# Reordering key sums, transposes and input copies, and giving GpSimd 144 of 384 columns of a product, in an attention and state-space kernel

## The chip, the cores and the metric

The kernel runs on one core of a Trainium2 chip. The metric is the device time of one execution in microseconds; the median of several executions is compared. Engine names are those of the profile: PE is TensorE (PEld its weight loads), DVE is VectorE, ACT is ScalarE, POOL is GpSimd, SP is SyncE, which here issues all DMAs.

## The reference, cut to what matters

The input is 8 samples of 512 channels by 48 x 48 = 2304 positions, all float32. Two layers follow each other, each adding to its own normalised input: a causal linear attention with 8 heads, and a chain of four selective state-space blocks ("Mamba") of 128 channels each.

```python
x = x + _L0_conv_ref(_gn(x), Wq, bq, Wkv, bkv)      # layer 0
x = x + _L1_conv_ref(_gn(x), ...)                   # layer 1
# layer 0: Q = elu(q)+1, K = elu(k)+1
den = 1.0 / (einsum('nhld,nhld->nhl', Q, cumsum(K, axis=1)) + 1e-10)
S = S + k[..., :, None] * v[..., None, :];  o = einsum('nhk,nhkv->nhv', q, S)   # per position
# layer 1, four times (channels i*128 ..), each on its own 128 channels plus the last result:
xs = silu(causal_conv4(u @ Wi_x.T) + bc);  z = u @ Wi_z.T
delta = softplus(dt @ Wdt.T + bdt);  A = -exp(A_log)
h = exp(delta * A) * h + (delta * xs) * B_t;  y_t = sum_n h * C_t               # per position, 256 x 16 states
x_m = ((y + xs * D) * silu(z)) @ Wo.T
fused = w_local * x_i + w_global * maximum(x_i, x_m)
```

Note the cumulative sum of K: the key as it comes out of its projection is summed by head over the heads' channels and over what lies before, and is multiplied with the query.

## The kernel before, in words

**Tiling.** Positions are cut into six chunks of 384 (`LC`). Layer 0 is a list of 8 x 4 x 6 = 192 calls of `chunk` (sample, group of 128 channels, chunk of positions). Layer 1 is a list of 192 jobs (class `Job`): sample, block, chunk of positions. Two streams of samples alternate, so that while one stream's job is scanned, the next one of the other is prepared.

**A job and its slots.** A job's 256 channels x 16 states are scanned in 8 slots (`SLOTS`) of 4 scans. Channels come in halves of 128: slots 0 to 3 are half 0, slots 4 to 7 half 1. A slot goes as follows. The product u = B x (delta xs) is made in two parts: `last_product` (L857) lets POOL make the last `TAIL` = 128 columns of each of the four rows (L864), `product` (L872) lets DVE make the first 256 (L875), which read delta xs from a copy in PSUM, `dxp`, that ACT makes in `inputs` (L845, L848) once per half from the loaded tile `dxr`. Then four scans on DVE (`scan`, L896) each take one decay row exp(delta A), which ACT has written to a PSUM bank (`decay`, L885). Then POOL multiplies with C (`weigh`, L908), and PE sums over states into the PSUM tile `yp` (`gather`, L924). `skip` (L850, L853) starts a half's sum: ACT writes xs x D over `yp`, which DVE must have read before (`gated`, L936, tile `yz`).

**The order is written out by hand.** `slot(k)` (L1145) issues what belongs to slot k: first the DVE product of slot k+1, then `gated` if it is due (half 1 of the job before at s = 2, half 0 at s = 6), then the background work of this half slot (`beside(2k)`), then four times: a scan, in slots 2 and 6 after the first one the `skip`, and `ahead(DEPTH)`, which issues decays until 3 are in hand. After the second scan come the copies of the last columns (`keep`, L919), one `gather`, `inputs`, `last_product` of slot k+2, and the second half's background work, `beside(2k+1)`. At s = 6 it is the `inputs(0)` of the next job, at s = 2 the `inputs(1)` of this one. At s = 7 the DVE product of the next job's slot 1 is issued here too, right after slot 7's second scan.

**Background work** is a set of generators: `chunk` for layer 0, `Job.prepare` (L688) for the next jobs, statistics, and the hand-over between blocks (`pass_on`). Each `yield` names the half slot at which the next step is due and how many PSUM banks it needs. In `chunk`, `at(j)` means j half slots after the chunk's start; in `prepare`, `first` is the half slot at which its job is first scanned. A chunk's start lies, for nearly all chunks, 3 half slots after a job's start. So a step at `at(9)` falls into the first half of slot 6, `at(10)` into its second half, and the job being prepared has `first - 21` in the second half of slot 5 (first convolution, L700), `first - 19` in the second half of slot 6 (second convolution and gate, L700 and L711) and `first - 18` at the start of slot 7 (four Silus, L736 to L741, between two loads of ACT's function tables). A softplus (L771) has two more loads.

**Banks.** Six PSUM banks (`BANKS`) are shared by the decays (3 to 5), the projections, the transposes and the convolutions. A bank is handed out in the program's order; whoever writes it next waits for who read it last.

**Queues that matter here.** Each engine runs its instructions in the order of issue. SP issues the loads of `prepare`: `steps` (dr), `scaled` (dxr), `rows` (B and C), two DMAs each, after `spread` has stored `delta` and `dx` to DRAM; `save`d stores are flushed at certain points. In a chunk, `kc` are the key sums (L381, L383), `kept` their copy for the next group (L387), `pr` the product with the query on DVE (L391), `turned` the transposed keys and values (L398), `kl` and `v` their copies to SBUF by ACT (L402, L403).

Of the kernel before, what the change touches and what calls it, by code (L numbers as in the profile page):

```python
# [19 lines left out]
LC = 384  # L20
NG = 2
SLOTS = 8
TAIL = 128
BANKS = 6
DEPTH = 3
LEAD = 11
# [24 lines left out]
def attention_then_mamba_kernel(  # L51
# [12 lines left out]
    nc = tc.nc  # L64
# [17 lines left out]
    ident = cst[:, C_ID : C_ID + P]  # L82
# [3 lines left out]
    k_tri = cst[:, C_TRI : C_TRI + P]  # L86
# [86 lines left out]
    def save(out, in_):  # L173
        stores.append((half_no[0], out, in_))

    def flush(every=True):
        while stores and (every or stores[0][0] <= half_no[0] - 2):
            _, o, i = stores.pop(0)
            nc.sync.dma_start(out=o, in_=i)
# [103 lines left out]
    def chunk(m):  # L283


        b, o, c = parts[m]
        n = f"{b}_{o}_{c}"
        bank = Banks()
# [5 lines left out]
        def at(j, gap=1):  # L294
            return times[m] + j, gap

        def new(tag, bufs=1, shape=(P, LC)):
            return apool.tile(list(shape), F32, tag=tag, name=f"{tag}_{n}", bufs=bufs)

        def project(j):  # L300
            ps = bank()[:, 0:LC]
            for kt in range(4):
                nc.tensor.matmul(  # L303
                    ps,
                    wqs[m // NC][:, kt, j * P : (j + 1) * P],
                    xn[:, kt, :],
                    start=(kt == 0),
                    stop=(kt == 3),
                )
            return ps, bqkv_sb[:, j * 4 + o : j * 4 + o + 1]  # L310
# [42 lines left out]
        if o:  # L353
            before = new("before")
# [14 lines left out]
        k = new("k", 2)  # L369
        nc.vector.scalar_tensor_tensor(k, ex, 1.0, kp, ALU.min, ALU.add)  # L370
        bank.free()
        yield at(4, 0), 1
        vp, vb = project(2)
        yield at(6), 0
        vT = new("vT")
        nc.scalar.activation(vT, vp, AF.Identity, bias=vb)
        bank.free()

        yield at(7), 1
        kc = bank()[:, 0:LC]  # L380
        nc.tensor.matmul(kc, k_tri, k, start=True, stop=(o == 0))  # L381
        if o:
            nc.tensor.matmul(kc, ident, before, start=False, stop=True)  # L383
        yield at(8), 0
        if ksum is not None:
            kept = new("before")
            nc.scalar.copy(kept[64:128], kc[64:128])  # L387
            save(ksum[:, cols], kept[64:128])
        yield at(9), 0
        pr = new("pr")  # L390
        nc.vector.tensor_mul(pr, q, kc)  # L391
        bank.free()
        yield at(9, 0), 2
        turned = []
        for src in (k, vT):
            ps = bank()[:, 0:LC].rearrange("p (i t) -> p i t", i=NT)
            for i in range(NT):
                nc.tensor.transpose(ps[:, i, :], src[:, subs[i]], ident)  # L398
            turned.append(ps)
        yield at(10), 0  # L400
        kl, v = new("kl", 1, (P, NT, P)), new("v", 2, (P, NT, P))
        nc.scalar.copy(kl, turned[0])  # L402
        nc.scalar.copy(v, turned[1])  # L403
# [42 lines left out]
        for sc in scs:  # L446
# [4 lines left out]
                start=True,  # L451
                stop=False,
                skip_group_check=True,
            )
        for i in range(NT):
            for h, sc in zip(heads_of, scs):
# [4 lines left out]
                    start=False,  # L461
                    stop=i == NT - 1,
# [12 lines left out]
        for i in range(NT):  # L475
            old = c > 0 or i > 0
            for h, sm in zip(heads_of, sms):
                if old:
# [4 lines left out]
                        start=False,  # L483
                        stop=False,
                        skip_group_check=True,
                    )
            for h, sm in zip(heads_of, sms):
# [4 lines left out]
                    start=False,  # L492
                    stop=i == NT - 1,
# [187 lines left out]
    class Job:  # L681
# [6 lines left out]
        def prepare(self):  # L688
# [3 lines left out]
            wk, s = self.w = st.w  # L692
            self.state, self.fsum, self.fm = st.state, st.fsum, st.fm
            xi, c0 = st.xi, c * LC
            bank = Banks()
# [28 lines left out]
            first = 2 * self.start  # L724
# [64 lines left out]
            def pairs(t, rows):  # L789
                for i in range(2):  # L790
                    nc.sync.dma_start(out=t[i * 64 : i * 64 + 64], in_=rows)

            def steps(h):
                self.dr[h] = drs[h]
                pairs(self.dr[h][:, :, 1 : 1 + LC], dsrc[h])

            def scaled(h):
                self.dxr[h] = mpool.tile([P, 2, LC], F32, tag="dxr", name=f"dxr_{n}_{h}")
                pairs(self.dxr[h], xsrc[h])

            def rows(m, q):
                t = mpool.tile([P, NG, LC], F32, tag="BC"[m], name=f"{'BC'[m]}_{n}_{q}", bufs=4)
                for i in range(2):
                    nc.sync.dma_start(  # L804
                        out=t[i * 64 : i * 64 + 64].rearrange("p j l -> p (j l)"),
                        in_=src[q, m, i].partition_broadcast(64),
                    )
                (self.B, self.C)[m][q] = t
# [8 lines left out]
            yield first - 7, 0  # L817
            flush()
            steps(0)
            rows(0, 0)  # L820
            yield first - 6, 0
            scaled(0)
            yield first - 5, 0
            rows(0, 1)
            self.prepared = True
# [19 lines left out]
        def inputs(self, h):  # L845

            self.dxp = psx.tile([P, 2, LC - TAIL], F32, tag="dxp", name=f"dxp_{self.n}_{h}")
            nc.scalar.copy(self.dxp, self.dxr[h][:, :, 0 : LC - TAIL])  # L848

# [7 lines left out]
        def last_product(self, s):  # L857

            shape, cols = [P, NG, 2, TAIL], slice(LC - TAIL, LC)
            u = mpool.tile([P, NG, 2, 1 + LC], F32, tag="u", name=f"u_{self.n}_{s}", bufs=5)  # L860
            if self.c:
                h, q = s // 4, s % 4 * NG
                nc.scalar.copy(u[:, :, :, 0], self.state[:, h, q : q + NG, :])
            nc.gpsimd.tensor_tensor(  # L864
                u[:, :, :, 1 + LC - TAIL :],
                self.B[s % 4][:, :, cols].unsqueeze(2).to_broadcast(shape),
# [5 lines left out]
        def product(self, s, u):  # L872

            shape, cols = [P, NG, 2, LC - TAIL], slice(0, LC - TAIL)
            nc.vector.tensor_mul(  # L875
                u[:, :, :, 1 : 1 + LC - TAIL],
                self.B[s % 4][:, :, cols].unsqueeze(2).to_broadcast(shape),
# [104 lines left out]
    slots = SLOTS * len(jobs)  # L982
# [45 lines left out]
    def finale(job):  # L1028
        yield "0", 1
        job.project()  # L1030
        yield "1", 0
        job.maximum()
        if job.c == NC - 1:
            yield from job.stream.pass_on()
# [4 lines left out]
    for b in counted:  # L1039
        first = times[parts.index((b, 0, 0))]  # L1040
# [23 lines left out]
    def beside(half):  # L1064

        half_no[0] = half
        flush(every=False)
        begin(half // 2 + LEAD)

        for t in heads:  # L1070
            if t.need is not None and t.need[1] == 0 and t.fits() and t.due():
                t.step()
        held = False
        for t in tasks + heads:
            while t.need is not None and t.due():
                if not t.fits() or held and t.need[1]:
                    held = held or t.need[1] > len(spare)
                    break
                t.step()
        prune()  # L1080
# [19 lines left out]
    def at(k):  # L1100
        return jobs[k // SLOTS], k % SLOTS

    def apart(k):

        return k % SLOTS == 0 and k > 0 and at(k)[0].c == 0 and at(k)[0].stream is at(k - 1)[0].stream
# [5 lines left out]
    def ahead(n):  # L1111

        nonlocal todo
        while len(decays) < n and spare and todo < 4 * slots:
            k = todo // 4
            if apart(k) and k not in primed:
                break
            job, s = at(k)
            if not job.prepared or s // 4 not in job.dr:
                break  # L1120
            decays.append(job.decay(s, todo % 4))
            todo += 1
# [22 lines left out]
    def slot(k):  # L1145
        job, s = at(k)
        end = k + 1 == slots or apart(k + 1)
        if not end and k + 1 not in drawn:
            j, r = at(k + 1)
            j.product(r, us[k + 1])  # L1150
        before = jobs[k // SLOTS - 1] if k >= SLOTS else None
        if s == 2 and before is not None and not before.closed:
            before.gated(1)
            tasks.insert(0, Task(finale(before)))
        elif s == 6:
            job.gated(0)
        beside(2 * k)
        for i in range(4):
            job.scan(s, i, us[k], decays.pop(0))
            if i == 0 and s in (2, 6):  # L1160
                job.skip(s // 4)
            ahead(DEPTH)
            if i == 1:

                while kept:
                    kept.pop(0)()
                if len(waiting) > 1:
                    waiting.pop(0)()
                if s == 2:
                    job.inputs(1)  # L1170
                elif s == 6 and k + 2 < slots and not apart(k + 2):
                    j = at(k + 2)[0]
                    if not j.prepared:
                        hurry(k + 2, lambda: j.prepared)
                    j.inputs(0)
                if not end and k + 2 < slots and not apart(k + 2):
                    j, r = at(k + 2)
                    us[k + 2] = j.last_product(r)
                    if s == 7:

                        j.product(r, us[k + 2])
                        drawn.add(k + 2)
                beside(2 * k + 1)
        u = us[k]
        job.weigh(s, u)
        kept.append(lambda: at(k)[0].keep(s, u))
        waiting.append(lambda: at(k)[0].gather(s, us.pop(k)))
        if end:
            close(k)
            if k + 1 < slots:  # L1190
                prime(k + 1)
            else:
                hurry(slots, lambda: not tasks)
                flush()
# [101 lines left out]
```

## Time and profile before

| | |
|---|---|
| median of 3 runs | 8580.44 us (8571.5 to 8580.68) |
| the profiled execution | 8565.29 us, its span 8563.5 us |
| busy: PE, DVE, ACT, POOL | 7704.4, 8067.9, 6845.7, 7758.3 us |
| scans (L896), 6144 | 5457.8 us busy, 940 ns each |
| decays (L885), 6144 | 3412.3 us busy, 578 ns each |
| ACT table loads (L885, L736, L771) | 1283 ns each, 192 of L736 |
| idle of PE ahead of the convolutions (L700) | 215.6 us, of which 163.1 until ACT's copy kl |
| TensorE clock granted | 0.973 of full |

The page gives busy time by engine, then groups of equal instructions: line, engine, operation, tile written <- tiles read, size, count; after the first bar the busy time in us and the mean of one in ns; after the second the engine's idle time just before, and what ended most of it. Consecutive DVE and ACT instructions overlap by some tens of ns, so count times mean is a little over the busy time. The table of waits reads: engine, tile and line that waited, <- what ended the wait: us in total, times, longest. The timeline gives start, length, instruction, and in brackets the idle time ahead of it. The profiled execution is one execution; it was 15 us under the median.

### The profile page before, as it was taken

What the parts mean: (1) busy time and instruction counts of PE and PEld (TensorE: products, weight loads), DVE (VectorE), ACT (ScalarE), POOL (GpSimd) and SP (SyncE); (2) the same over time, 40 slices, a digit from 0 to 9 for tenths busy, and PEclk for the clock granted to TensorE, in tenths of its full rate; (3) what the DMA queues carried; (4) which work ended last, traced back from release to release, by engine and by line L of the source; (5) the groups of instructions that cost most, each with busy time, mean ns of one, the idle gap of its engine ahead of it and who ended that gap; (6) DMA issues with size and microseconds to landing.
All of it is one profiled execution on the core that took longest, in us unless ns stands there. A gap on an engine that the chain in (4) does not pass through costs nothing. (4 is left out here: it accounts for less than half of the span.)

```text
span 8563.5 us, 124248 instructions
## 1 busy us (share of the span) xinstructions
PE 7704.4 (90%) x36482; PEld 3691.2 (43%) x36482; DVE 8067.9 (94%) x11078; ACT 6845.7 (80%) x14438; POOL 7758.3 (91%) x4235
## 2 busy tenths in 40 slices
PE   8899999999999999999899999999899999999975
PEld 4444444444444444444444444444444444444422
DVE  2899999999999999999999999999999999999998
ACT  3788888878888888878888888888788888888875
POOL 1789999999999999999999999999999999999998
PEclk9999999999999999999999999999999999999977
DMA  5667777767766777777777677777777676666665
GB/s 186 172 185 191 200 203 195 201 194 203 207 192 190 198 202 204 200 192 197 200 203 196 192 190 203 202 200 194 199 202 201 192 194 190 187 191 190 180 162 148
DMA packets 974424, 1654.36 MB, mean 193 GB/s; under 512 B 119337, under 2 KB 768169, under 8 KB 973618
## 3 DMA queue, kind: packets, MB, share of 16 engines
q1 hardware_dynamic: 973746, 1646.43, 69.8%
q8 instruction: 290, 4.75, 0.2%
q14 instruction: 388, 3.18, 0.1%
HBM read 1318.28 MB, written 327.68 MB: 192 GB/s over the span
## 5 line engine op out<-in xcount | busy, mean ns | idle before, releaser
L896 DVE TENSOR_TENSOR_SCAN u<-bank,u 128x385 f32<-128x385 f32 (+1 forms) x6144 | 5457.8, 940 | 254.2 <-ACT bank L885 253.8
L908 POOL TENSOR_TENSOR u<-u,C 128x1536 f32<-128x1536 f32 x1536 | 4889.0, 3183 | 606.8 <-DVE u L896 284.9
L885 ACT ACTIVATE bank<-dr,scales 128x385 f32<-128x385 f32 (+1 forms) x6144 | 3412.3, 578 | 700.6 <-DVE u L896 598.1
L924 PE MATMUL yp<-u,cst 128*64 128x384 f32 x12288 | 2368.3, 506 | 176.5 <-POOL u L908 91.3
L864 POOL TENSOR_TENSOR u<-B,dxr 128x512 f32<-128x512 f32 x1536 | 1965.5, 1280 | 19.6 <-DMA dxr<-xscr 17.0
L875 DVE TENSOR_TENSOR u<-B,dxp 128x1024 f32<-128x1024 f32 x1536 | 1837.7, 1196 | 10.0 <-ACT dxp L848 10.0
L303 PE MATMUL bank<-xn,wq 128*128 128x384 f32 x4608 | 1721.9, 518 | 66.3 <-DVE u L896 41.3
L924 PEld LDWEIGHTS yp<-u,cst 128*64 128x64 f32 x12288 | 773.4, 138 | 1365.7 <-issue 897.5
L700 PE MATMUL bank<-xi,wk 128*128 128x384 f32 x3072 | 1123.9, 509 | 215.6 <-ACT kl L402 163.1
L303 PEld LDWEIGHTS bank<-xn,wq 128*128 128x128 f32 x4608 | 862.0, 197 | 837.9 <-DVE u L896 128.4
L700 PEld LDWEIGHTS bank<-xi,wk 128*128 128x128 f32 x3072 | 563.5, 193 | 780.5 <-ACT kl L402 274.1
L315 ACT ACTIVATE ex<-bank,bqkv_sb 128x384 f32<-128x384 f32 x384 | 221.0, 576 | 447.5 <-PE bank L303 447.5
L885 ACT ACT_TABLE_LOAD x382 | 490.1, 1283 | 6.8
L853 ACT ACTIVATE yp<-xs,scales 128x384 f32<-128x384 f32 x384 | 223.4, 582 | 316.7 <-DVE yz L936 316.7
L813 POOL TENSOR_TENSOR dx<-delta,xs 128x384 f32<-128x384 f32 x384 | 385.5, 1004 | 22.3 <-ACT delta L771 22.3
L435 PE MATMUL bank<-cst,rdb 128*128 128x128 f32 x576 | 100.7, 284 | 262.0 <-DVE u L896 260.0
L942 PE MATMUL bank<-yz,scales 128*128 128x384 f32 x768 | 303.2, 511 | 32.4 <-DVE yz L936 21.3
L760 PE MATMUL bank<-dbc,steps_w 9*128 9x384 f32 x768 | 301.2, 511 | 3.0 <-ACT dbc L752 3.0
L711 PE MATMUL bank<-xi,scales 128*128 128x384 f32 x768 | 288.6, 497 | 11.0 <-ACT xs L736 11.0
L747 PE MATMUL bank<-xs,scales 128*40 128x384 f32 x768 | 280.8, 488 | 2.7 <-ACT sm L469 2.7
L488 PE MATMUL bank<-sm,v 128*64 128x128 f32 x2304 | 256.0, 301 | 0.0
L736 ACT ACT_TABLE_LOAD x192 | 246.3, 1283 | 3.5
(117 smaller groups left out, 7866.5 us busy)
## 6 DMA issues: line engine op xcount, KB each, us to landing
B<-scr SPq DMA_DIRECT2D x1536, 192.0 KB, 4.3
C<-scr SPq DMA_DIRECT2D x1536, 192.0 KB, 4.7
xn<-xn SPq DMA_DIRECT2D x192, 768.0 KB, 7.1
dr<-dscr SPq DMA_DIRECT2D x768, 192.0 KB, 3.8
dxr<-xscr SPq DMA_DIRECT2D x768, 192.0 KB, 4.9
dscr<-delta SPq DMA_DIRECT2D x192, 384.0 KB, 6.8
xscr<-dx SPq DMA_DIRECT2D x192, 384.0 KB, 2.4
xn<-in_x SPq DMA_DIRECT2D x48, 768.0 KB, 6.4
```

The source lines that it names most:

```text
L303: nc.tensor.matmul(ps, wqs[m // NC][:, kt, j * P : (j + 1) * P], xn[:, kt, :], start=(kt == 0), stop=(kt == 3),)
L700: nc.tensor.matmul(xc, wk[:, k, h * P : (h + 1) * P], xi[:, c0 + k : c0 + k + LC], start=(k == 0), stop=(k == 3),)
L711: nc.tensor.matmul(zp, w_gate[:, s, h * P : (h + 1) * P], xi[:, c0 + 3 : c0 + 3 + LC], start=True, stop=True,)
L760: nc.tensor.matmul(vp, steps_w[32:41, s, h * P : (h + 1) * P], dbc[32:41, :], start=True, stop=True)
L813: nc.gpsimd.tensor_tensor(dx[:, h, :], delta[:, h, :], xs[:, h, :], ALU.mult)
L864: nc.gpsimd.tensor_tensor(u[:, :, :, 1 + LC - TAIL :], self.B[s % 4][:, :, cols].unsqueeze(2).to_broadcast(shape), self.dxr[s // 4][:, :, ...
L875: nc.vector.tensor_mul(u[:, :, :, 1 : 1 + LC - TAIL], self.B[s % 4][:, :, cols].unsqueeze(2).to_broadcast(shape), self.dxp.unsqueeze(1).to ...
L885: nc.scalar.activation(dA[:, cols], self.dr[h][:, g, cols], AF.Exp, scale=w_a[:, self.w[1], 2 * h + g, q + j : q + j + 1],)
L896: nc.vector.tensor_tensor_scan(u[:, j, g, cols], dA[:, cols], u[:, j, g, cols], 0.0, ALU.mult, ALU.add,)
L908: nc.gpsimd.tensor_tensor(u[:, :, :, 0:LC], u[:, :, :, 1:], self.C[s % 4].unsqueeze(2).to_broadcast([P, NG, 2, LC]), ALU.mult,)
L924: nc.tensor.matmul(self.yp[g * 64 : g * 64 + 64, 0:LC], pair_sum, u[:, j, g, 0:LC], start=False, stop=(s % 4 == 3 and j == NG - 1), skip_g ...
L942: nc.tensor.matmul(self.xm[:, 0:LC], w_out[:, self.w[1], h, :], self.yz[:, h, :], start=(h == 0), stop=(h == 1),)
```

## The change

`TAIL` goes from 128 to 144: POOL makes 144 columns of each row of the product with B, DVE 240, and `dxp` is two rows of 240.

In `chunk` the key sums move from `at(7)` to `at(5)`, ahead of vT's bias on ACT; the copy `kept` follows vT at `at(6)` (before: `at(8)`); `pr` moves from `at(9)` to `at(7)`, the transposes from `at(9, 0)` to `at(7, 0)`, and the copies `kl` and `v` from `at(10)` to `at(9)`, the first half of slot 6.

In `prepare` the load of the first `dxr` moves from `first - 6` to `first - 7`, and the first rows of B from `first - 7` to `first - 6`.

In `slot`, at s = 6, the next job's `inputs(0)` is issued after the first scan and ahead of `skip`, if that job is prepared by then; otherwise after the second scan, as before.

```diff
-TAIL = 128
+TAIL = 144
...
         yield at(4, 0), 1
         vp, vb = project(2)
+        yield at(5), 1
+        kc = bank()[:, 0:LC]
+        nc.tensor.matmul(kc, k_tri, k, start=True, stop=(o == 0))
+        if o:
+            nc.tensor.matmul(kc, ident, before, start=False, stop=True)
         yield at(6), 0
         vT = new("vT")
         nc.scalar.activation(vT, vp, AF.Identity, bias=vb)
         bank.free()
-
-        yield at(7), 1
-        kc = bank()[:, 0:LC]
-        nc.tensor.matmul(kc, k_tri, k, start=True, stop=(o == 0))
-        if o:
-            nc.tensor.matmul(kc, ident, before, start=False, stop=True)
-        yield at(8), 0
         if ksum is not None:
             kept = new("before")
             nc.scalar.copy(kept[64:128], kc[64:128])
             save(ksum[:, cols], kept[64:128])
-        yield at(9), 0
+        yield at(7), 0
         pr = new("pr")
         nc.vector.tensor_mul(pr, q, kc)
         bank.free()
-        yield at(9, 0), 2
+        yield at(7, 0), 2
         turned = []
...
-        yield at(10), 0
+        yield at(9), 0
         kl, v = new("kl", 1, (P, NT, P)), new("v", 2, (P, NT, P))
...
             yield first - 7, 0
             flush()
             steps(0)
+            scaled(0)
+            yield first - 6, 0
             rows(0, 0)
-            yield first - 6, 0
-            scaled(0)
...
             if i == 0 and s in (2, 6):
+                j = at(k + 2)[0] if s == 6 and k + 2 < slots and not apart(k + 2) else None
+                early = j is not None and j.prepared
+                if early:
+                    j.inputs(0)
                 job.skip(s // 4)
...
-                elif s == 6 and k + 2 < slots and not apart(k + 2):
+                elif s == 6 and not early and k + 2 < slots and not apart(k + 2):
```

## The prediction

> **What bounds the kernel now.** I read the page's engine line and groups first, then who waited for whom, then the timeline of one job (eight slots of four scans) engine by engine, then the busy time of whole jobs.
>
> ```profile
> PE 7704.4 (90%) x36482; PEld 3691.2 (43%) x36482; DVE 8067.9 (94%) x11078; ACT 6845.7 (80%) x14438; POOL 7758.3 (91%) x4235
> ...
> L908 POOL TENSOR_TENSOR u<-u,C 128x1536 f32<-128x1536 f32 x1536 | 4889.0, 3183 | 606.8 <-DVE u L896 284.9
> ...
> L864 POOL TENSOR_TENSOR u<-B,dxr 128x512 f32<-128x512 f32 x1536 | 1965.5, 1280 | 19.6 <-DMA dxr<-xscr 17.0
> L875 DVE TENSOR_TENSOR u<-B,dxp 128x1024 f32<-128x1024 f32 x1536 | 1837.7, 1196 | 10.0 <-ACT dxp L848 10.0
> ```
>
> DVE is the fullest engine. Its 495.6 us of idle time are the start (about 180), and this, from the table of waits:
>
> ```profile
> ACT yp L853 <- DVE yz L936: 316.7, 203, 3.5
> DVE u L896 <- ACT bank L885: 253.8, 192, 3.8
> PE bank L700 <- ACT kl L402: 163.1, 161, 1.7
> ```
>
> The scans wait for a decay 192 times, and there are 192 jobs: one stop of 1.32 us in each. The timeline shows its place; first DVE, then ACT, same job:
>
> ```profile
> 2572.19 0.55 DVE L936 TENSOR_TENSOR yz<-yp,sz 128x384 f32<-128x384 f32 x1
> 2572.66 0.54 DVE L391 TENSOR_TENSOR pr<-q,bank 128x384 f32<-128x384 f32 x1
> 2573.12 3.50 DVE L896 TENSOR_TENSOR_SCAN u<-bank,u 128x385 f32<-128x385 f32 x4
> 2576.54 1.20 DVE L875 TENSOR_TENSOR u<-B,dxp 128x1024 f32<-128x1024 f32 x1
> ...
> 2583.57 2.66 DVE L896 TENSOR_TENSOR_SCAN u<-bank,u 128x385 f32<-128x385 f32 x3 [1.68 <-ACT bank L885]
> ```
>
> ```profile
> 2572.78 0.58 ACT L853 ACTIVATE yp<-xs,scales 128x384 f32<-128x384 f32 x1 [1.47 <-DVE yz L936]
> ...
> 2575.66 0.58 ACT L848 COPY dxp<-dxr 128x512 f32<-128x512 f32 x1
> 2576.18 0.19 ACT L863 COPY u<-state 128x4 f32<-128x4 f32 x1
> 2576.39 0.48 ACT L402 COPY kl<-bank 128x384 f32<-128x384 f32 x1
> 2576.77 0.49 ACT L403 COPY v<-bank 128x384 f32<-128x384 f32 x1
> 2577.14 1.11 ACT L885 ACTIVATE bank<-dr,scales 128x385 f32<-128x385 f32 x2
> 2578.27 1.28 ACT L736 ACT_TABLE_LOAD   x1
> ```
>
> The reader is to see: ACT sits idle for 1.47 us ahead of the skip term, then does dxp, kl and v, and only then the two decays and the switch to Silu. From the load at 2578.27 to the last scan of slot 7 at 2583.57 lie 5.30 us in which ACT delivers nothing that DVE can scan with; DVE's own work ends 1.68 us short of that. So the length of a job (42.6 to 42.7 us in most) is set by a loop: DVE up to the last scan of slot 6, then ACT through the Silu stage. Two other engines stand close. Busy time of two whole jobs:
>
> ```profile
> 2552.60:2595.30 42.70, 39.20 (x192) 18.87 (x192) 40.92 (x55) 35.99 (x80) 38.94 (x21) 1.00 0.72 195
> 2120.00:2162.60 42.60, 38.83 (x193) 18.61 (x192) 41.16 (x61) 35.20 (x71) 42.40 (x27) 1.00 0.58 161
> ```
>
> Columns from the third: PE, weight load, DVE, ACT, POOL. In the usual job POOL has 3.8 us to spare (39 to 40 us busy in seven of ten jobs); in the second kind, where it also normalises chunks for a new sample, 0.2. I count 38 jobs of 41.4 us or more.
>
> **What the Trainium skill says.** (1) "GPSIMD Engine Reference", Elementwise side-by-side cycle accounting: a two-input op costs about 2.6 cycles an element at 1.2 GHz, 2.17 ns. The trace agrees: 730, 1004 and 1280 ns for 256, 384 and 512 elements (L543, L813, L864) are 2.15 ns each more; only L908 is flatter (1.86 from 512 to 1536). (2) The same page, Key points: GpSimd and VectorE contend where a DVE instruction has two SBUF inputs. Here the DVE product reads dxp from PSUM, and L864 keeps within 1251 to 1328 ns, so the trace shows little of it. (3) "ScalarE: Activation LUTs", What ACT_TABLE_LOAD costs: 1283 ns, the trace's 1283; its further drain of 1380 ns does not show, Silu starts 1.29 us after the load (2579.56).
>
> **The change, part by part.** *144 columns for GpSimd.* 64 elements leave the DVE product. From yz (384: 552 ns) to the product (1024: 1196 ns), both with a PSUM input, is 1.006 ns an element: 64.4 ns x 1536 = **98.9 us off DVE**. POOL gets 64 x 2.15 = 137 ns x 1536 = 211 us (low end 1.86 ns: 183; high end in proportion to 1280/512: 246), so 1.10 us a job (0.95 to 1.28). In the usual job this lies in the 3 to 4 us of spare; in the full ones it is on the path. The dxp copies shorten by 24 ns each (581 for 512 against 484 for 384), 9 us of ACT: counted as nothing.
>
> *Copies and inputs ahead of the skip term.* In the built order of the changed kernel, ACT does kl, v, dxp, skip, then decay, decay, state copies, decay, decay, table load, in nearly every job. kl and v (0.86 us back to back) fit the 1.47 us in which ACT stood idle. dxp must wait until the DVE product ahead of yz has read the old dxp (2572.19), so it ends some 0.1 us after yz; the skip behind it, and PE's gather behind that, are late by that much, and the next decay only has to be there for the scan 2.6 us later. If that cover is gone dxp costs 0.58. The fourth decay takes the bank of slot 6's last scan, so it starts at 2576.6 and not at 2577.7; the load follows at 2577.2, not 2578.27: **1.07 us earlier**. DVE has 0.13 us less to do in that stretch (two products), so its wait shrinks by at most 0.94. Read job by job from the trace, the waits are 1.7 us in a quarter of the jobs, 0.3 to 1.5 in most others; the sum of the smaller of wait and 0.94 is **157 us**.
>
> *What is late next.* PE runs without a gap from slot 2 to the second convolution, whose 1.20 us wait for kl (2576.93) goes: kl's and v's banks are no longer the ones it takes. Without it the convolution ends 1.2 us earlier (2578.4), the second Silu is wanted at 2577.2 + 1.28 + 0.48 = 2579.0. It fits by 0.6.
>
> *Key sums and transposes moved.* The same matmuls, 6 transposes and 2 to 4 passes a chunk, in front of other matmuls; DVE's pr moves from slot 6 to slot 5, still before slot 6's last scan: nothing. Six banks are full in slot 5 and no longer in slot 6; decays then wait for scans there, with three in hand: nothing. ACT's copy of the key sums now follows vT directly; PE has the sums about 0.4 to 1 us before. If not, up to 0.8 us (L383's pass), on ACT alone.
>
> *Moved loads.* The dxr pair (2 DMAs of 0.6 us on SP) goes ahead of the first B pair and closer behind the xscr store (2.4 us to landing): SP may wait under 1 us; the B rows are issued 1.3 us later, with some 10 us before POOL reads them. ACT reads dxr about 3.5 us earlier; it was issued 6.7 us before yz ended and lands 4.9 us after issue: hidden by about 2 us, and the issue is itself 1.2 us earlier.
>
> *POOL's price.* New usual job: 42.7 - 0.39 (six products) - 1.07 = 41.2; POOL 39.9 + 1.1 = 41.0, just under. The 38 full jobs and the last few need 43 to 43.5 where DVE would need 41.2 to 42: 68 us if no job lends time to the next, 38 if a backlog of 3 us is carried (the lag that the mid-job slots show already). I take 50.
>
> **Sum:** 98.9 + 157 - 50 = 206 us. The profiled execution took 8565.3 (span 8563.5): it would take 8360. The median of the runs, 8580.4, is 15 us above it; less 205 it is **8375**.
>
> **The rivals.** (a) *POOL takes DVE's place in most jobs.* For: 41.0 against 41.2 leaves nothing for the waits at L908 that come in the middle of a job (slot 2: about 1.2 us). Against: full jobs ran with 0.2 us idle. With 1 us of it kept, 42.1 a job: some 110 us saved, 8470. (b) *PE or something else holds the Silu stage*: the second convolution follows gather of slot 4, which waits for a POOL that is now later; then half of the 157 comes and POOL's loss stays: 8455. (c) *Slower: a 576-element product costs POOL far more.* It decides from (43.4 - 40.4 - 0.5) / 8 = 0.31 us more a product (mean job, POOL's mean, idle kept), twice the slope. At 0.40, 44.1 a job, 0.7 x 191 = 140 us more: 8720. For it: four rows of 144 have not been seen. Against: three sizes on one line. (d) No loss on POOL at all: 8320. That the change does not do what it says is excluded for the order, which is built so.
>
> **How the numbers follow.** Forecast 0.55 (8330 to 8415), (a) 0.20, (b) 0.13, (c) 0.08, (d) 0.04. The range 8320 to 8490 leaves out (c) and the ends of (a) and (d). About 0.2% (17 us) is what a measurement can tell from no change; faster by more 0.88, within 0.04 (tails of (a) and (b)), slower 0.08.
>
> **What would show it.** Product on DVE near 1132 ns, tail on POOL near 1417. The wait of scans for decays under 110 us; that of the second convolution for kl gone; skip's wait for yz down by half. Job lengths near 41.3, and 43 where chunks are normalised, POOL over 95% busy. Wrong if POOL's tail is above 1450 ns, if decays still wait over 200 us, or if DVE waits for yz or for POOL's tail.

## The result and the profile after

| | before | after |
|---|---|---|
| median | 8575.97 us (8564.56 to 8580.68, 4 runs) | 8491.56 us (8486.39 to 8496.54, 4 runs) |
| ratio | | 0.9903, 95% interval 0.9886 to 0.9921 |
| profiled execution (span) | 8565.29 (8563.5) | 8496.54 (8494.8) |

84 us were gained and 205 forecast; the range 8320 to 8490 just misses it. First the page of the kernel after: the engines, then the groups that answer to those of before (the lines of the code have moved up by two).

```profile
PE 7704.6 (91%) x36482; PEld 3689.3 (43%) x36482; DVE 7987.4 (94%) x11078; ACT 6879.1 (81%) x14437; POOL 7962.5 (94%) x4235
...
L906 POOL TENSOR_TENSOR u<-u,C 128x1536 f32<-128x1536 f32 x1536 | 4902.3, 3192 | 292.3 <-DVE u L894 96.6
L862 POOL TENSOR_TENSOR u<-B,dxr 128x576 f32<-128x576 f32 x1536 | 2188.5, 1425 | 47.2 <-DMA B<-scr 37.8
...
L873 DVE TENSOR_TENSOR u<-B,dxp 128x960 f32<-128x960 f32 x1536 | 1729.2, 1126 | 30.4 <-DMA B<-scr 24.3
```

Both prices came as forecast: 108.5 us off the DVE product (forecast 98.9), 145 ns more for each POOL product (forecast 137), 204 us more on POOL in all. But DVE's busy time fell by 80.5 us (the lengths of all its instructions fell by 120.9, but in the records they overlap each other by 40 us less) and the span by 68.7: DVE idles 12 us more than before, where the forecast had 107 us less (157 at the decays, 50 given back to POOL). The table of waits of the kernel after says for what (a row is: who waited <- what ended the wait: us in total, times, longest):

```profile
DVE u L894 <- ACT bank L883: 193.0, 198, 5.2
...
PEld bank L376 <- ACT sm L467: 136.6, 165, 4.3
...
ACT dxp L846 <- DMA dxr<-xscr: 59.1, 53, 8.7
...
PE bank L376 <- ACT sm L467: 48.5, 94, 3.6
...
ACT xs L737 <- PE bank L698: 42.3, 115, 2.7
...
ACT sz L739 <- PE bank L709: 28.8, 172, 1.5
...
ACT yp L851 <- DVE yz L934: 13.9, 9, 4.0
```

The wait of the skip term for yz is gone (316.7 before), and so is the second convolution's for kl (TensorE's idle time ahead of the convolutions fell from 215.6 to 28.0 us). Yet the scans still wait 193.0 us for decays, where the prediction named 110. New: the Silu stage waits 71.1 us for PE (its two rows, 42.3 for the convolution and 28.8 for the gate; before, 14.5 and 17.1), and the key sums (L376), now two half slots earlier, take a bank which ACT is still emptying: PE stands 48.5 us for it. The same two rows of the kernel before:

```profile
ACT sz L741 <- PE bank L711: 17.1, 105, 0.7
...
ACT xs L739 <- PE bank L700: 14.5, 16, 2.3
```

Where the time went is best read by kind of job, from the first scan of each job in the traces. "Full" are jobs 36 to 48, 85 to 96, 132 to 144 and 181 to 191, in which POOL also normalises chunks or finishes the output (a wider count than the prediction's 38 and the last few).

| us in the profiled execution | before | after | after less before | forecast, spread by jobs |
|---|---|---|---|---|
| ahead of the first scan | 224.0 | 222.3 | -2 | 0 |
| jobs 0 to 4 | 230.7 | 274.5 | **+44** | -7 |
| 49 full jobs | 2140.9 | 2158.1 | **+17** | -15 |
| 138 ordinary jobs | 5967.8 | 5839.8 | **-128** | -184 |

(The last column spreads 98.9 + 157 over 192 jobs, and puts the 50 on the full ones.) So three things are to be explained: 51 us in the first five jobs, 32 in the full ones, 56 in the ordinary ones.

**The first jobs.** Busy time of jobs 0 to 4 of the kernel after, columns as in the prediction, and two lines of its timeline at the end of job 1:

```profile
222.29:496.80 274.51, 219.54 (x1002) 105.89 (x1000) 206.28 (x280) 180.36 (x375) 189.50 (x93) 0.91 0.52 141
```

```profile
322.62 0.56 ACT L846 COPY dxp<-dxr 128x480 f32<-128x480 f32 x1 [8.72 <-DMA dxr<-xscr]
...
324.26 1.15 DVE L873 TENSOR_TENSOR u<-B,dxp 128x960 f32<-128x960 f32 x1 [20.43 <-DMA B<-scr]
```

DVE has no more to do than before (206.28 against 207.75) in 44 us more time: it stood 20.43 us for the first B rows of job 2, whose preparation had come too late.

**An ordinary job.** The timeline of the kernel after, PE first, then ACT, same job:

```profile
3087.26 2.85 PE L698 MATMUL bank<-xi,wk 128*128 128x384 f32 x8
3090.04 1.51 PE L922 MATMUL yp<-u,cst 128*64 128x384 f32 x8
3091.48 2.85 PE L698 MATMUL bank<-xi,wk 128*128 128x384 f32 x8
3094.17 1.45 PE L709 MATMUL bank<-xi,scales 128*128 128x384 f32 x4
```

```profile
3092.27 1.28 ACT L734 ACT_TABLE_LOAD   x1
...
3094.37 0.58 ACT L737 ACTIVATE xs<-bank,scales 128x384 f32<-128x384 f32 x1 [0.22 <-PE bank L698]
...
3095.66 0.49 ACT L739 ACTIVATE sz<-bank 128x384 f32<-128x384 f32 x1 [0.15 <-PE bank L709]
...
3097.46 1.09 ACT L883 ACTIVATE bank<-dr,scales 128x385 f32<-128x385 f32 x2
```

Each PE line begins before the one ahead of it has ended: both convolutions, the gather between them and the gate products run without a gap, and the second and the fourth Silu each wait for the end of such a block. ACT no longer stands for yz ahead of this, but the stage behind the table load now runs at PE's pace. The kernel before had the last of these waits already, in the very job that the prediction took (PE, then ACT):

```profile
2579.61 1.50 PE L711 MATMUL bank<-xi,scales 128*128 128x384 f32 x4
```

```profile
2581.15 0.49 ACT L741 ACTIVATE sz<-bank 128x384 f32<-128x384 f32 x1 [0.15 <-PE bank L711]
```

In all 192 jobs of both kernels the fourth Silu starts only when the gate products have ended. Over the 138 ordinary jobs, the traces give these means; the first three rows count from the end of slot 6's last scan:

| us | before | after | change | forecast |
|---|---|---|---|---|
| the Silu table load starts | 1.56 | 0.65 | -0.92 | -1.07 |
| the second convolution ends | 3.16 | 2.65 | -0.51 | -1.2 |
| the gate products end | 4.49 | 3.94 | -0.55 | left out |
| from the table load to the end of the fourth Silu | 3.46 | 3.83 | **+0.37** | 0 |
| scans' wait for decays, 138 jobs together | 163.6 | 106.7 | **-57** | -113 |
| the rest of the time of these jobs, together | 5804.2 | 5733.1 | -71 | -71 |

(113 and 71 are 157 and 98.9 times 138/192.) So the shorter DVE product paid in full in these jobs, and the whole of what is missing is wait: the load came almost as early as forecast, but PE's last product did not come with it.

### The profile page after: what moved, and what is told of

It reads as the page before. It is cut to its first block, busy times and chain, and to the rows that moved or that the text cites. A ratio compares the mean times of both kernels' runs of the same rounds, so it can differ in the third digit from the quotient of the medians.

```text
span 8494.8 us, 124303 instructions
## 1 busy us (share of the span) xinstructions
PE 7704.6 (91%) x36482; PEld 3689.3 (43%) x36482; DVE 7987.4 (94%) x11078; ACT 6879.1 (81%) x14437; POOL 7962.5 (94%) x4235
## 5 line engine op out<-in xcount | busy, mean ns | idle before, releaser
L894 DVE TENSOR_TENSOR_SCAN u<-bank,u 128x385 f32<-128x385 f32 (+1 forms) x6144 | 5450.7, 937 | 196.6 <-ACT bank L883 193.0
L922 PE MATMUL yp<-u,cst 128*64 128x384 f32 x12288 | 2396.7, 511 | 297.2 <-POOL u L906 170.7
L862 POOL TENSOR_TENSOR u<-B,dxr 128x576 f32<-128x576 f32 x1536 | 2188.5, 1425 | 47.2 <-DMA B<-scr 37.8
L303 PE MATMUL bank<-xn,wq 128*128 128x384 f32 x4608 | 1709.5, 515 | 89.5 <-POOL xn L327 44.0
L873 DVE TENSOR_TENSOR u<-B,dxp 128x960 f32<-128x960 f32 x1536 | 1729.2, 1126 | 30.4 <-DMA B<-scr 24.3
L303 PEld LDWEIGHTS bank<-xn,wq 128*128 128x128 f32 x4608 | 856.7, 196 | 846.5 <-DVE u L894 138.2
L698 PE MATMUL bank<-xi,wk 128*128 128x384 f32 x3072 | 1104.6, 502 | 28.0 <-POOL xi L672 26.0
L698 PEld LDWEIGHTS bank<-xi,wk 128*128 128x128 f32 x3072 | 556.5, 191 | 574.4 <-issue 98.4
L433 PE MATMUL bank<-cst,rdb 128*128 128x128 f32 x576 | 106.7, 297 | 213.4 <-DVE u L894 209.8
L846 ACT COPY dxp<-dxr 128x480 f32<-128x480 f32 x384 | 216.2, 563 | 85.4 <-DMA dxr<-xscr 59.1
```

The lines of the kernel that those rows point to most:

```text
L303: nc.tensor.matmul(ps, wqs[m // NC][:, kt, j * P : (j + 1) * P], xn[:, kt, :], start=(kt == 0), stop=(kt == 3),)
L698: nc.tensor.matmul(xc, wk[:, k, h * P : (h + 1) * P], xi[:, c0 + k : c0 + k + LC], start=(k == 0), stop=(k == 3),)
L862: nc.gpsimd.tensor_tensor(u[:, :, :, 1 + LC - TAIL :], self.B[s % 4][:, :, cols].unsqueeze(2).to_broadcast(shape), self.dxr[s // 4][:, :, ...
L873: nc.vector.tensor_mul(u[:, :, :, 1 : 1 + LC - TAIL], self.B[s % 4][:, :, cols].unsqueeze(2).to_broadcast(shape), self.dxp.unsqueeze(1).to ...
L894: nc.vector.tensor_tensor_scan(u[:, j, g, cols], dA[:, cols], u[:, j, g, cols], 0.0, ALU.mult, ALU.add,)
L922: nc.tensor.matmul(self.yp[g * 64 : g * 64 + 64, 0:LC], pair_sum, u[:, j, g, 0:LC], start=False, stop=(s % 4 == 3 and j == NG - 1), skip_g ...
```

## The experiments

Every kernel is compared with the kernel before, run beside it. The parts in question: the **tail** (144 columns), the **chunk part** (key sums, pr, transposes, kl and v), the **inputs** (dxp ahead of the skip term, and the loads in `prepare`).

| run | median us | ratio, 95% interval | jobs 0-4 | full | ordinary | scans' wait for decays | Silu stage's wait for PE |
|---|---|---|---|---|---|---|---|
| before | 8574 to 8577 | 1 | 230.7 | 2140.9 | 5967.8 | 253.8 | 31.6 |
| after | 8491.56 | 0.9903 | 274.5 | 2158.1 | 5839.8 | 193.0 | 71.1 |
| 1: before + tail | 8534.9 | 0.9954 [0.9937, 0.997] | 230.7 | 2166.3 | 5908.5 | 278.8 | |
| 2: after, tail 128 | 8505.57 | 0.9917 [0.9902, 0.9932] | 274.7 | 2121.1 | 5890.0 | 136.5 | 44.6 |
| 3: after, first 12 chunks in old order | 8456.22 | 0.9862 [0.9847, 0.9876] | 229.1 | 2154.9 | 5847.2 | 186.7 | 70.6 |
| 4: 3 + filler in all jobs | 8452.11 | 0.9854 [0.984, 0.9869] | 235.1 | 2162.9 | 5818.9 | 179.6 | |
| 5: 3 without `before` | 8419.65 | 0.9818 [0.9802, 0.9835] | 229.6 | 2153.5 | 5806.8 | 147.5 | 37.8 |
| 6: 3, key sums one half slot later | 8733.26 | 1.018 [1.0165, 1.0196] | 238.2 | 2182.8 | 6087.9 | 337.9 | |
| 7: before + chunk part | 8509.84 | 0.9921 [0.9906, 0.9936] | 275.6 | 2116.8 | 5900.1 | 116.4 | |
| 8: before + inputs | 8492.23 | 0.9901 [0.9886, 0.9916] | 230.0 | 2127.9 | 5907.1 | 163.4 | 24.4 |
| 9: 8 + tail | 8493.38 | 0.9904 [0.9889, 0.9918] | 229.3 | 2158.5 | 5873.5 | 219.6 | 41.8 |
| 10: 3, tail 128 in full jobs | 8413.25 | 0.9811 [0.9795, 0.9828] | 230.3 | 2118.5 | 5837.0 | 166.0 | |
| 11: 9, tail 128 in full jobs | 8459.18 | 0.9864 [0.9849, 0.9878] | 229.6 | 2126.9 | 5874.3 | | |
| 12: 10 + filler in ordinary jobs | 8383.74 | 0.9778 [0.9765, 0.9791] | 228.3 | 2118.8 | 5809.7 | 155.3 | |

Job times and waits are those of each run's one profiled execution; only medians carry an interval.

### 1 and 2: the tail alone, and all but the tail

```diff
-TAIL = 128
+TAIL = 144
```

> The kernel before with 144 columns for GpSimd, nothing moved. Theory (a job's length is set by a loop, DVE up to slot 6's last scan and then ACT through the Silu stage; two of the eight DVE products lie beside the Silu stage and their shortening buys nothing): 6 x 0.064 us x 191 jobs = 74 us come off, and the jobs with a full GpSimd give back about 45: some 8546 us, ratio 0.9965, and the wait of scans for decays grows to about 280 us. Rival (DVE is the bound, each of the eight products counts): 99 - 45, 8522 us, ratio 0.994, wait unchanged.

8534.9: between the two. It gains 59 us in the ordinary jobs and loses 25 in the full ones. DVE's busy time fell by 85.5 us, but the scans' wait for decays *rose* by 25, as the theory had it. The place is another, though: only 7 of the 25 us lie in the ordinary jobs, 17 in the full ones.

Run 2 is the change with `TAIL = 128`.

> The changed kernel with 128 columns as before. Theory (jobs 1 to 4 lose 44 us because the moved chunk steps lock up the six banks; ordinary jobs gain about 0.4 us from the moves): jobs 1 to 4 take about 55 us each again, the rest gains 75: some 8545 us, ratio 0.9965. Rival (the early loss comes with the longer GpSimd product): jobs 1 to 4 as before, 8500 us, ratio 0.991.

8505.57, near the 8500 that the rival gave, but not for its reason: the loss in the first five jobs is all there (274.7 us), so it does not come with POOL's longer product. The moves gain 78 us in ordinary jobs and 20 in full ones. Between run 2 and the change, 16 columns more are worth 50 us in the ordinary jobs and cost 37 in the full ones.

### 3: the first 12 chunks in the old order

```diff
+        late = m < 12
...
-        yield at(5), 1
+        if not late:
+            yield at(5), 1
+            kc = sums()
...
+        if late:
+            yield at(7), 1
+            kc = sums()
+            yield at(8), 0
...
-        yield at(7), 0
+        yield at(9 if late else 7), 0
...
-        yield at(9), 0
+        yield at(10 if late else 9), 0
```

> The changed kernel, but the first twelve chunks, which start every 11 half slots and not at the phase of the others, keep the old order of key sums, transposes and copies. Theory (the loss of the early jobs is the bank lock of these chunks): jobs 1 to 4 take 43 to 52 us as before, 44 us less than the changed kernel, 8447 us, ratio 0.985. Rival (the load order or the early inputs cause it): 8491, ratio 0.990.

8456.22, 35 us under the change (8447 was expected), and the first five jobs are back at their old length:

```profile
227.92:457.06 229.14, 207.81 (x1001) 102.52 (x1000) 205.32 (x280) 178.20 (x373) 189.39 (x93) 0.96 0.61 167
```

The reader is to see DVE, ACT and POOL as busy as in the kernel after, to within 2.2 us, in 45 us less. The first chunks start 11 half slots apart and not 16, so their steps fall into other half slots than the prediction looked at. That they lock up the six banks, so that job 2's preparation finds none, is argued from the order of the program; that the chunk part does it and the inputs do not is shown (run 7 has the loss, run 8 has not).

### 4: filling the pause of PE in slot 1

```diff
         yield at(16), 1
+        for _ in range(FILL):
+            nc.tensor.matmul(
+                yp[:, LC : LC + P], ident, ident, start=True, stop=True, skip_group_check=True
+            )
         rb = bank()[:, 0:LC].rearrange("p (i t) -> p i t", i=NT)
```

> As the late start, and ahead of the three transposes of the denominators PE does 8 idle matmuls of 128 columns into unused columns of the yp bank (about 1.2 us, in the place where PE sat idle for 1.5 us in slot 1). Theory (the record shows half the clock for 3.4 us after that idle time in 47 of 176 jobs, and those take 1.23 us longer): the half-clock stretches in slots 1 to 3 go, waits of q and k fall under 20 us, 8447 - 50 = 8397 us, ratio 0.979. Rival (the half clock isn't tied to that gap, and the matmuls only delay PE): 8447 or more.

8452.11: the rival's number. The trace shows more than the time does. Of the 4608 matmul records of the projections (L303 in run 3), those longer than 0.7 us fell from 207 to 20, and the ordinary jobs by 28 us; but start and first jobs took 12 and the full jobs 8 us more. So the effect is real and the filler was put into too many places; run 12 comes back to it.

### 5: less work for PE ahead of the gate

This kernel leaves out the sums over the earlier channel groups (`before`), so its output is another.

```diff
-            nc.tensor.matmul(kc, k_tri, k, start=True, stop=(o == 0))
-            if o:
-                nc.tensor.matmul(kc, ident, before, start=False, stop=True)
+            nc.tensor.matmul(kc, k_tri, k, start=True, stop=True)
```

> The changed kernel with its first 12 chunks in the old order (8456 us), and the sum over earlier column groups left out: the products of the identity with `before`, 0.81 us of TensorE in 144 of 192 chunks, in slot 4 (the outputs of three of four channel groups are then other values). Theory: from slot 4 to the gate product TensorE has no pause left, so the four Silu, the decays behind them and the last scan of slot 7 wait for it; 0.81 us less in three of four jobs takes about 0.5 us off that scan's wait of 0.9 us, the scans' wait for decays falls from 187 us to about 115, the time to about 8400 (0.980 of the kernel before). Rival: ScalarE's own queue or the table load holds that scan; the wait stays above 170 us and the time at 8446 or more (0.985).

8419.65. Two waits of run 3, then of run 5:

```profile
DVE u L905 <- ACT bank L894: 186.7, 196, 4.5
...
ACT xs L748 <- PE bank L709: 41.4, 112, 2.6
```

```profile
DVE u L903 <- ACT bank L892: 147.5, 164, 5.0
...
ACT xs L746 <- PE bank L707: 21.0, 38, 2.2
```

With 117 us of PE work taken out (the group of L380 in run 3, 288 records), the second Silu's wait for PE halves, the scans' wait falls by 39 us and the time by 37. It was to be 8400 by the theory, 8446 by the rival. The Silu stage's wait for PE fell by 33 us in all (70.6 to 37.8). In the ordinary jobs the stretch from the table load to the end of the fourth Silu went from 3.82 to 3.53 us, 40 us in 138 jobs, with the load where it was (0.65 us after slot 6's last scan in both), and these jobs became 40 us shorter: PE does hold the Silu stage. But only a third of the work taken away comes back as time; where the stage did not wait for PE, there was nothing to gain.

### 6: the key sums one half slot later

```diff
         if not late:
-            yield at(5), 1
+            yield at(6), 1
             kc = sums()
```

> As the changed kernel with its first 12 chunks in the old order (8456 us), but the key sums one half slot later than the change puts them (half slot 6, the half slot of the copy that reads them). In half slot 5 they take the bank that ScalarE's second Relu of the chunk ahead frees in that same half slot, and TensorE stands 49 us on it in all, ahead of the convolution and the gate. Theory: that stall goes, the Silu stage comes 0.2 to 0.3 us earlier, time about 8425 (0.982). Rival: one half slot later they take the bank of the values' projection, or their product with q on VectorE then waits for them; the wait changes its name only, time 8450 to 8475.

8733.26: 277 us worse than run 3, outside both expectations. The stall that it was to remove is gone from the table of waits, and another is in its place. From its timeline:

```profile
3358.99 0.81 PE L380 MATMUL bank<-before,cst 128*128 128x384 f32 x2
...
3359.83 0.47 ACT L396 COPY before<-bank 64x384 f32<-64x384 f32 x1 [2.48 <-PE bank L380]
...
3361.17 2.85 PE L709 MATMUL bank<-xi,wk 128*128 128x384 f32 x8
...
3364.38 0.48 ACT L411 COPY kl<-bank 128x384 f32<-128x384 f32 x1 [1.16 <-PE bank L407]
...
3366.36 1.51 PE L933 MATMUL yp<-u,cst 128*64 128x384 f32 x8 [1.69 <-ACT yp L862]
```

One half slot later, the key sums are issued behind the chunk's attention products (3355.2 to 3358.2), and the transposes (L407) behind the convolution. ACT then stands 2.48 us for the sums and 1.16 us for the transposes, with decays and the skip term queued behind, and PE's gather waits 1.69 us for that skip: two queues, each waiting for the other. In the table of waits, PE's gather for the skip went from 111.3 us (run 3) to 364.3, kl for the transposes from 6.1 to 285.5. So the bank that the key sums wait for in the change (48.5 us of PE) is the cheaper evil.

### 7 and 8: the two moves, each alone

Run 7 is the kernel before with the diff of `chunk`, run 8 the kernel before with the diffs of `prepare` and `slot`.

> The kernel before with the chunk's part of the change alone: key sums, transposes and copies of keys and values earlier, GpSimd's share still 128 columns, inputs copied after the skip term. Theory, that each of two holds is enough to keep the Silu stage late (ScalarE behind the skip term, TensorE's convolution behind the key copy): the start loses its 44 us and the other jobs gain little, 10 us; time about 8605 (1.0035). Rival, that the parts add: two thirds of the 97 us that both moves gain after the start belong to the key and value copies, so 44 lost and 65 gained, about 8553 (0.9975).

> The kernel before with the inputs copied ahead of the skip term and their loads a half slot earlier, GpSimd's share still 128 columns, chunks in the old order. Theory, that each of two holds keeps the Silu stage late: no loss at the start, and only about 15 us gained, 8560 (0.998). Rival, that the parts add: a third of 97 us, 8542 (0.996). If the early loads or the input's wait for its load cost something, slower than 8574.

8509.84 and 8492.23: both theories fall. In ordinary jobs the chunk part alone gains 68 us, the inputs alone 61, both 78 (run 2). Neither is needed for the other, and they do not add. Both shorten one loop, the chunk part by freeing PE's convolution from the key copy and ACT from kl and v ahead of the table load, the inputs by taking the dxp copy out from there. The traces show why they do not add: counted from slot 6's last scan as above, the table load comes 0.75 us earlier in run 7, 0.54 in run 8 and 0.92 with both (run 2), but the gate products end 0.64, 0.56 and 0.70 us earlier. Either move alone brings PE nearly as far as both, and the Silu stage ends with PE. In the ordinary jobs the scans' wait for decays fell by 100, 76 and 94 us in these three runs, but the rest of the time rose by 32, 15 and 16. A part of that may be TensorE's clock: 53, 52 and 49 of the 138 jobs had a stretch at half of it in slots 1 to 3 (last section), against 33 before; this was not tried by itself. The inputs alone are worth as much as the whole change, since they lose nothing at the start.

### 9, 10 and 11: what the tail pays, and where

Run 9 is run 8 with `TAIL = 144`. Runs 10 and 11 give each job a tail of its own:

```diff
+            j = start // SLOTS
+            full = 36 <= j < 49 or 85 <= j < 97 or 132 <= j < 145 or j >= 181
+            self.tail = 128 if full else TAIL
```

> The kernel before with the early input copies and their loads and with 144 columns on GpSimd, all chunks in the old order: the change without its chunk part. Theory: the two moves stand in for each other (84 us by the inputs alone, 67 by the chunks alone with 44 lost at the start, 71 by both), so the chunk part adds next to nothing, and the shorter product adds the 40 us that it is worth alone: 8452 (0.9855), the same within 10 us as the change with its first 12 chunks in the old order. Rival: the shorter product pays only as far as the chunk part has brought the convolution forward (TensorE waits 0.4 us a job for the key copy without it): 8475 or more (0.988).

> The changed kernel with its first 12 chunks in the old order (8456 us), and GpSimd's share back at 128 columns in 49 of the 192 jobs, those in which GpSimd also normalises a chunk of the next pass or finishes the output (jobs 36 to 48, 85 to 96, 132 to 144 and from 181). Theory: these jobs last as long as GpSimd's work, which 144 columns make 1.1 us longer, so they fall by 7 to 10 us a group, 34 us in all: 8422 (0.982). Rival: GpSimd's wait is hidden there too and VectorE's longer product costs what it saves elsewhere, 0.5 us a job: 8456 to 8480.

> The early inputs and the 144 columns with all chunks in the old order, and 128 columns in the same 49 jobs. Theory: the two effects add, 8452 less 34 us, 8418 (0.9815), as good as any kernel here. Rival: with the old chunk order the jobs with a GpSimd-normalised chunk wait for the key copy instead, and less than 15 us comes back: 8440 or more.

Run 9: 8493.38, no better than run 8. Its theory falls: against run 8 the ordinary jobs gain 34 us, the full ones lose 31. Run 10: 8413.25, 43 us under run 3; run 11: 8459.18, 34 under run 9. That answers for the full jobs. Jobs 36 to 48 in run 3 (144 columns), then in run 10 (128):

```profile
1778.24:2348.50 570.26, 516.89 (x2457) 245.60 (x2456) 542.99 (x746) 466.22 (x984) 560.43 (x321) 0.97 0.72 202
```

```profile
1778.53:2339.56 561.03, 518.02 (x2457) 244.66 (x2456) 547.16 (x747) 466.71 (x984) 548.16 (x321) 0.98 0.74 205
```

POOL (the seventh column) is down by 12.3 us, the stretch by 9.2, while DVE is up by 4.2: in these jobs POOL sets the time. Runs 10 and 11 differ by the chunk part alone, which is worth 46 us in the medians and 37 in the ordinary jobs at 144 columns, but only 17 at 128 (runs 8 and 2).

### 12: tails by job and filler where it pays

This is run 10 with the filler of run 4, cut to the ordinary jobs:

```diff
+        job = half_no[0] // (2 * SLOTS)
-        for _ in range(FILL):
+        for _ in range(FILL if job >= 5 and not full(job) else 0):
```

> The kernel with the first 12 chunks in the old order and 128 columns in the 49 full jobs (8413 us), and in the other jobs from the sixth on eight idle products of 128 columns into an unused part of yp, where TensorE pauses 1.2 us in slot 1 (they change no result). With them in every job the projection of the queries ran at half clock in 20 products in place of 207, the ordinary jobs fell by 29 us in all, and start and full jobs rose by 20. Theory: the pause is followed by 3.4 us at half clock in one job of four, which makes such a job 1.2 us longer; the gain of 29 us stays and the loss doesn't: 8387 (0.978). Rival: the filler takes elsewhere on TensorE what it saves, or the 29 us lay between executions: 8407 or more (0.9805).

8383.74, as the theory had it: 0.9778 of the kernel before, and the fastest here. Long records of L303's kind fell from 196 (run 10) to 82, the ordinary jobs by 27 us.

## Why the prediction was wrong, point by point

- **Both prices** (64 elements off DVE, on POOL) were right: 108.5 for 98.9 us, 145 for 137 ns. The 2.17 ns an element of "GPSIMD Engine Reference", Elementwise side-by-side cycle accounting, is confirmed to 5% (145 / 64 = 2.27).
- **"One stop of 1.32 us in each" job, shortened by an earlier table load: right in kind, too large.** The load came 0.92 us earlier. But the stage behind it became 0.37 us longer, and DVE had 0.14 us less to do in that stretch (two products): that leaves 0.41 us a job, the 57 us by which the waits of the ordinary jobs fell in place of 113. The step that failed is *What is late next*, "It fits by 0.6". It compared the end of the second convolution with the second Silu in one job, and left out the gate products right behind, on which the stage ends. In that job the convolution less 1.2 us ends at 2578.6 (2576.93 + 2.85 - 1.2; it says 2578.4). The gate products ended at 2581.11; 1.2 us earlier is 2579.9, just when the fourth Silu would want them (2577.2 + 1.3 + 3 x 0.48): nothing to spare, even by its own numbers. And 1.2 us was the wait for kl in that one job; over the ordinary jobs it was 0.83 us on average (114.4 us in slot 6). PE's second convolution came 0.89 us earlier in a job, but DVE reached the end of slot 6's last scan 0.38 us earlier, too; against that scan the convolution gained the 0.51 us of the table. Run 5 shows that PE work taken out ahead of the gate comes back as time. This is rival (b), PE holding the Silu stage, at 8455; run 3, the change without its loss at the start, took 8456. That the totals agree so well is partly chance, and the reason given there (a gather that POOL makes late) is not what the trace shows: in the ordinary jobs of the kernel after, PE's waits for POOL's u (those over 0.15 us) come to 0.4 us in all in slots 2 to 7.
- **The sum.** 98.9 us less DVE work and 157 us less wait were added, with 0.13 us a job taken off for the two products beside the Silu stage. The first came in full in the ordinary jobs. But PE does not keep up with a quicker DVE: with 16 columns more on top of the moves (run 2 to the change) DVE reaches the end of slot 6's last scan 0.51 us earlier in a job, PE its second convolution only 0.30. The Silu stage grew from 3.67 to 3.83 us and the scans' wait in the ordinary jobs by 37 us, from run 8 to run 9 by 43. So there the tail was worth 50 us on top of the moves, not 71.
- **"Key sums and transposes moved ... nothing", "Six banks are full in slot 5 ... nothing": wrong at the start.** With chunks 16 half slots apart it cost little (PE stands 29 us for the bank of the key sums in the ordinary jobs); the first 12 are 11 apart, and there it cost 44 us, shown by runs 3, 7 and 8.
- **POOL's price: right in mechanism, low in size.** 50 us of POOL less 98.9 x 49/192 = 25 of DVE should have cost the full jobs 25; from run 2 to the change the tail costs them 37, and runs 10 and 11 get 36 and 32 us of it back. The moves, too, gained only 20 us there, where 157 x 49/192 = 40 were counted: the scans' wait for decays in these jobs fell by 25 us only (78.0 to 53.1).
- **Moved loads: right** in ordinary jobs. dxp waits for its load 59.1 us in all, 15.2 of them in the first five jobs; the job shown above 0.49 us.

What stays open: the exact step at which the banks lock at the start, and why the moves gained only half of what was counted in the full jobs; POOL was busy for 95% of these jobs before, but that it is the reason is not shown.

## What to carry to other kernels

When several engines lie within a few per cent of each other, gains on one loop do not add: after each step, ask for every engine that feeds the stage when its *last* product is due, not its first. Check an order that was read off a usual job against the jobs at the start, where the spacing differs. If work can be given to another engine, give it by job: the same 16 columns were worth 50 us in jobs where GpSimd had room, and cost 37 where it had none.

## What was not expected of the hardware

A short pause of PE can be followed by half its clock. In the kernel after, two lines of PE's timeline and the window of the second (length of the stretch, then busy time of PE, weight load, DVE, ACT and POOL, then the mean clock):

```profile
3105.40 0.52 PE L433 MATMUL bank<-cst,rdb 128*128 128x128 f32 x3 [1.48 <-DVE u L894]
...
3106.16 4.54 PE L303 MATMUL bank<-xn,wq 128*128 128x384 f32 x8 [0.24 <-DVE u L894]
```

```profile
3106.10:3110.80 4.70, 4.64 (x9) 2.53 (x10) 4.70 (x7) 3.25 (x8) 4.70 (x3) 0.64 1.06 279
```

The eight products take 4.54 us in place of 2.85 (the same shape, L698 above), at a mean clock of 0.64. The records show most such stretches (59 of 90) as 3.4 us at 0.5; they fell into slots 1 to 3 in 47 of 176 jobs (5 to 180), which took 43.00 us (median) where the others took 41.77; among the ordinary jobs alone, 30 of 138, the medians are the same. "TensorE: Matmul & The Clock Gate", The HAM clock gate, gives a free-running window of 3413 ns, which agrees; but it has the clock fall after an idle window of about that length, and here 1.5 us of pause in a stream otherwise 91% busy were enough at times. Eight idle products in the pause of each ordinary job (run 12: 286.7 us of PE's busy time in all) left such a stretch in slots 1 to 3 in 3 of the ordinary jobs, against 25 in run 10, and the ordinary jobs were 27 us shorter. In the full jobs and at the start the same filler cost 20 us (run 4); in the full jobs it also took none of the stretches away (27 jobs had one in run 3, 30 in run 4). Why, the runs do not show.
